# Another table of wanted times for a planned order: four layers of attention and experts on one core

## The chip, the cores and the metric

The kernel runs on one core of one Trainium2 chip. Its time is the device time of one execution in microseconds (us), and versions are compared by the median of several executions. A separate execution was taken with the hardware profiler, which records when each instruction of each engine starts and how long it takes. The engines are called PE (TensorE), DVE (VectorE), ACT (ScalarE), POOL (GpSimd) and SP (SyncE, which in this kernel issues nearly all DMAs).

## The reference

The input x has 64 sequences of 64 tokens of 128 values, the context has 64 sequences of 64 tokens of 96 values, all float32. Four layers follow one another, and each adds two updates to x: a cross-attention to the context and a mixture of experts.

```
for i in 0..3:
    x = x + tanh(g_xattn[i]) * attention_i(layernorm(x), ctx)
    x = x + tanh(g_ffn[i])   * experts_i(layernorm(x))
return x
```

- Layer 0: attention with 16 heads of 8 values; 32 small experts, of which each token takes 6, and a shared expert.
- Layer 1: attention with 16 heads, and a rule that holds for the whole batch: if any weight of the softmax is NaN, all weights become 1/64. Then 8 experts with 256 hidden values, of which each token takes 2, and a shared expert.
- Layer 2: attention with 8 heads of 64 values; 8 experts, two of them per token, and a shared expert.
- Layer 3: a resampler, in which x asks and the keys are the context (masked) and x itself, 2 heads with normalised queries and keys; 4 experts with a layer norm inside, two per token, and a layer norm of the result.

## The kernel before, in words

**Tiles.** The 4096 tokens are 32 tiles of 128, and these are 8 blocks of 512 tokens (`NB`, `TB`, `TOK`, lines 21 to 25). x stays in SBUF for the whole kernel. Work is done block by block: in the main loop (lines 1750 to 1789) each layer's attention or experts for one block is one *stage*. The stages have kinds: "16 heads, 0" and "16 heads, 1" (`attention_16`, line 760), "gated 0" and "gated 2" (`gated_ffn`, line 1340), "end of 16 heads, 1" (line 922), "context, 8 heads" (keys and values of layer 2, line 934), "8 heads" (line 971), "resampler" (`attention_lat`, line 1084), "last" (`ffn_3`, line 1684), and "gated 1" (`sparse_ffn`, line 1527), which takes two blocks at once, so that there are four of it, called groups 0 to 3. The end of layer 1's attention needs the flag of the NaN rule from all 8 blocks; so the first half of the program holds layers 0 and the attention of 1, and the second half the rest.

**Who sets the order.** The body does not issue instructions. It records them in a `Plan` (line 184): every call becomes an operation with an engine, an estimated duration, and what it reads and writes. `stage` (line 218) gives each operation a key, a wanted time that runs from the start to the end named for this stage in the table `TIMES` (lines 49 to 90), in step with the TensorE work in it:

```
op.key = start + (end - start) * done / total
if op.eng == "PE":
    done += op.us
```

`order` (line 288) then plays the program through with its estimates: whenever an engine is free it takes, among the operations that are ready and can hold their buffers, the one with the smallest key (on ACT a change of function table adds 3.0 to the key). At most two stages of a kind are open at a time (`at_once`; the two kinds of 16 heads count together, and so do "gated 0" and "gated 2"). `issue` (line 431) emits the operations in the order of these starts, each into its engine's queue; on the chip each engine runs its queue strictly in that order. As all instructions are emitted at line 435, all rows of the profile say L435, and the tiles' names tell the steps apart. TIMES has 72 pairs (8 per kind, 4 for "gated 1"). They are no promise of times: some of them lie before zero, or end before they start.

**The steps that the prediction names.** A layer norm leaves z (POOL or DVE); PE transposes it into pz, and ACT copies that to zTm or zTs (`normed_T`, line 659). From zT come the projections pq (queries), and pk and pv from the context. sc and sc8 are scores of 16 and 8 heads, pr8 the softmax of "8 heads", whose last step is two multiplications on POOL; pt are transposed softmax rows, av and av8 the attention output, which ACT copies to yT, and po its projection.

In "gated 0", "gated 2" and "last" every token meets every expert with a weight. The routing gives pl (logits), the weights are transposed (pcT), copied by ACT, stored to HBM (cD) and loaded again as rows spread over all partitions (pb; `weights_T` and `spread`, lines 1228 and 1238). g and u are the two hidden matmuls, h = silu(g) * u, weighted by pb on POOL, and acc collects the second matmul. In "last", pg are matmuls with a Gram matrix that give variances (pvar), zs are weighted inputs (DVE, from pb), ph the hidden matmuls, acc3 the sums.

"gated 1" is sparse. After the routing of two blocks, `slots_of` (line 1399) sorts tokens by expert into 24 tiles of 128 slots: PE makes ranks (prank), DVE works on them, PE makes the list of tokens (pid), and DVE writes it as z_rows. The shared expert runs meanwhile (g, u, h, acc). Then, for eight triples of tiles, SP fetches three experts' weights (wt, 384 KB a tile; at most three wt are held), POOL gathers three tiles of tokens (zs, 24 gathers a group), PE transposes them (pt), ACT copies them back to zs, and g, u, h, po follow; the result goes to HBM (oD):

```
for k, j in enumerate(js):
    fetch(wt[:, k, :, :].rearrange("p k w -> p (k w)"), w_rows[0:1, j : j + 1], expert_d)
for k, j in enumerate(js):
    gather(zs[:, k, :], zD, z_rows[:, j : j + 1])
```

At a group's end POOL gathers each token's two results (back, 16 gathers a group), and DVE adds them to x. "8 heads" of the same blocks follows. It loads its keys and values (kT8, v8, 1 MB each), which "context, 8 heads" had stored.

Of the kernel before, what the change touches and what calls it, by code (L numbers as in the profile page):

```python
# [47 lines left out]

TIMES = {
    "16 heads, 0": [  # L50
        (-246, 241.8), (90, 178.8), (206.3, 259), (345.6, 219),
        (400.2, 417.7), (451.6, 497.5), (524.8, 338.3), (616.8, 153.4),
    ],
    "16 heads, 1": [
        (115.4, 151.3), (255.3, 431.1), (-4.4, 256.7), (501.1, 574.1),
        (-154.1, 516.8), (645.4, 766.1), (725.5, 820.9), (327.2, 1815.9),
    ],
    "8 heads": [
        (1810.8, -289.4), (1215.1, 808.1), (1395.5, 939.2), (1485.1, 876.8),
        (756.1, 1010.9), (1771.2, 1176.9), (1150.1, 1706.2), (1641.6, 1363.8),  # L60
    ],
    "context, 8 heads": [
        (-1505.7, -266.7), (1321.7, 960), (268.1, 103.1), (1421.2, 860.9),
        (851.2, 615.6), (1214.3, 1438.8), (1351.2, 821.5), (1428.4, 903.1),
    ],
    "end of 16 heads, 1": [
        (549.1, -654.8), (774.2, -702.6), (2005.6, 1294.3), (527.8, 1272.9),
        (1973.5, 1999.7), (1128.7, 3466.8), (2201.7, 2327.6), (1453, 882.6),
    ],
    "gated 0": [  # L70
        (199, 245.1), (223.9, 304.3), (284.5, 327.4), (374, 492.2),
        (446, 533.4), (593.6, 598.8), (598.3, 694.5), (646.3, 779.7),
    ],
    "gated 1": [
        (-153.1, 570.4), (771.2, 898), (1240.1, 1502.8), (1569.3, 1755),
    ],
    "gated 2": [
        (-544.7, 789.1), (1046.6, 1080.4), (-523.3, 690.8), (-176.3, 1324.9),
        (765.4, 1282.7), (432.2, 1488.7), (111.2, 1616), (1389.7, 2013.7),
    ],  # L80
    "last": [
        (994.7, 1236.8), (1107.1, 1287.4), (1101.4, 1732.7), (853.8, 1150.1),
        (1753.5, 2380.6), (2351, 2461.2), (2622.5, 2971), (-245, -130.7),
    ],
    "resampler": [
        (-824.7, 580.6), (285.1, 510.5), (781.7, 32.2), (1559.7, 1223.5),
        (-1333.4, 131.4), (-54.8, -881.9), (1140.3, 81.7), (-280.5, -1539.5),
    ],
}
AT_ONCE = {}  # L90
# [1797 lines left out]
```

## Time and profile before

| what | value |
|---|---|
| times of five runs | 1733.81, 1726.38, 1719.09, 1724.93, 1730.34 us |
| their median | 1726.38 us |
| time of the profiled execution | 1730.04 us |
| its span, first to last instruction | 1728.3 us |
| mean granted clock of TensorE | 0.961 |
| instructions | 37,328 |
| PE busy | 1587.6 us, 92% of the span, 14,369 matmuls |
| DVE, POOL, ACT busy | 1064.2 (62%), 930.5 (54%), 859.0 us (50%) |
| function table loads on ACT | 159, 204.0 us |
| DMA | 180.94 MB, 105 GB/s in the mean |

"Busy" is the time in which an engine carries out an instruction; what is left of PE's span, 140.7 us, is idle. The page also cuts the span into 40 slices of 43.2 us and gives for each the busy tenths of every engine and the clock that TensorE was granted (9 is 0.9 or more; full speed is 1). A row of the trace names the start, the duration, the engine, the operation, the tile written and the tile read, and in brackets the idle time before it with the engine and tile that ended it. The view of waits sums these by pair: total, number, longest.

### The profile page before, as it was taken

To read this page: it belongs to the slowest core of one execution; us is meant where nothing else is said; L and a number is where in the kernel's file an instruction comes from. 1 tells how busy PE (TensorE), PEld (TensorE's weight loads), DVE (VectorE), ACT (ScalarE), POOL (GpSimd) and SP (SyncE) were. 2 spreads that over 40 slices of the span, in tenths; PEclk is the share of its full clock that TensorE was granted. 3 is DMA by queue.
4 is the path that set the end of the run, shared out by engine and by line. 5 is a ranking of instruction groups with operands and counts; after the bars stand their busy time and mean duration, and the time that the engine had idled before them with its cause. 6 is when DMAs were issued, how large, how long until landed. Compare 5 with 4: busy or idle time off the path is not lost. (4 is left out here: it accounts for less than half of the span.)

```text
span 1728.3 us, 37328 instructions
## 1 busy us (share of the span) xinstructions
PE 1587.6 (92%) x14369; PEld 1095.3 (63%) x14369; DVE 1064.2 (62%) x2933; ACT 859.0 (50%) x1289; POOL 930.5 (54%) x906
## 2 busy tenths in 40 slices
PE   6999999999999999977769599999999999899976
PEld 3556556556566666556758487766767786677654
DVE  4864777786678665761746366684655474675652
ACT  3563776666757575622324264444443553454332
POOL 7464555565654745322373555686554566654741
PEclk9999999999999999987879799999999999999998
DMA  7231160324031321464567362521152323220201
GB/s 233 95 118 60 59 195 23 117 100 118 27 123 33 102 81 55 159 203 118 150 218 212 97 216 53 181 95 57 37 160 88 103 62 109 88 91 2 81 32 38
DMA packets 107786, 180.94 MB, mean 105 GB/s; under 512 B 22964, under 2 KB 53016, under 8 KB 103128
## 3 DMA queue, kind: packets, MB, share of 16 engines
q1 hardware_dynamic: 102488, 168.06, 29.9%
q0 software_dynamic: 5120, 10.50, 2.9%
q8 instruction: 113, 1.85, 0.4%
q14 instruction: 65, 0.53, 0.1%
HBM read 146.71 MB, written 35.26 MB: 105 GB/s over the span
## 5 line engine op out<-in xcount | busy, mean ns | idle before, releaser
L435 DVE TENSOR_TENSOR h<-h,u 128x512 f32<-128x512 f32 x224 | 150.8, 684 | 211.4 <-PE u L435 139.6
L435 POOL TENSOR_TENSOR h<-h,pb 128x512 f32<-128x512 f32 x128 | 161.6, 1276 | 198.1 <-DVE h L435 112.0
L435 ACT ACTIVATE h<-g 128x512 f32<-128x512 f32 x224 | 132.7, 597 | 226.1 <-PE g L435 201.4
L435 ACT ACT_TABLE_LOAD x159 | 204.0, 1283 | 28.6 <-issue 7.5
L435 POOL TENSOR_TENSOR ln_r<-ln_ve,minus_half 128x4 f32<-128x4 f32 x64 | 66.3, 1036 | 216.6 <-DVE ln_ve L435 206.7
L435 PEld LDWEIGHTS acc<-w_L,h 128*128 128x128 f32 x1088 | 134.9, 191 | 42.2 <-issue 30.4
L435 PEld LDWEIGHTS acc<-L_w,h 128*128 128x128 f32 x1088 | 133.5, 192 | 33.8 <-issue 24.1
L435 PE MATMUL acc<-w_L,h 128*128 128x128 f32 x1088 | 144.1, 278 | 0.8 <-POOL h L435 0.6
L435 PE MATMUL acc<-L_w,h 128*128 128x128 f32 x1088 | 142.7, 279 | 1.0 <-DVE h L435 0.4
L435 PE MATMUL g<-zTm,w_L 128*128 128x512 f32 x272 | 141.8, 604 | 0.5 <-ACT cn L435 0.5
L435 PE MATMUL u<-zTm,w_L 128*128 128x512 f32 x272 | 140.1, 599 | 0.0
L435 DVE TENSOR_REDUCE top<-sc 128x16 f32<-128x1024 f32 x80 | 97.4, 1218 | 63.4 <-PE sc L435 32.3
L435 POOL TENSOR_TENSOR kb<-kT,masks 128x1024 f32<-128x1024 f32 x64 | 121.1, 1907 | 23.5 <-ACT kT L435 8.1
L435 POOL DMA_INDIRECT zs<-zD,z_rows x96 | 92.9, 967 | 75.3 <-DVE z_rows L435 23.7
L435 POOL TENSOR_SCALAR z<-x,ln_mv,ln_r 128x128 f32<-128x128 f32 x160 | 128.6, 817 | 4.4 <-DMA zs<-cT 0.7
L435 ACT COPY prT<-pt 128x512 f32<-128x512 f32 x176 | 96.0, 592 | 50.0 <-PE pt L435 44.0
L435 POOL TENSOR_TENSOR pb<-zTm,pb 128x512 f32<-128x512 f32 x64 | 80.1, 1274 | 43.7 <-DMA pb<-cD 43.5
L435 ACT ACTIVATE pr<-pr 128x1024 f32<-128x1024 f32 x88 | 93.0, 1057 | 17.0 <-DVE pr L435 16.2
L435 PEld LDWEIGHTS pt<-masks,pr 128*128 128x128 f32 x704 | 79.9, 142 | 31.8 <-issue 21.7
L435 PE MATMUL pt<-masks,pr 128*128 128x128 f32 x704 | 97.4, 276 | 2.9 <-POOL pr L435 1.1
L435 POOL TENSOR_TENSOR pr<-pr,rs 128x512 f32<-128x512 f32 (+1 forms) x40 | 47.9, 1214 | 80.5 <-DVE rs L435 58.5
L435 POOL DMA_INDIRECT back<-oD,rows_of x64 | 63.5, 992 | 45.1 <-issue 23.8
(299 smaller groups left out, 3382.6 us busy)
## 6 DMA issues: line engine op xcount, KB each, us to landing
wt<-experts SPq DMA_DIRECT2D x96, 384.0 KB
pb<-cD SPq DMA_DIRECT2D x256, 128.0 KB
pb<-cD SPq DMA_DIRECT2D x96, 256.0 KB
k_d<-kS SPq DMA_DIRECT2D x8, 1024.0 KB
v_d<-vS SPq DMA_DIRECT2D x8, 1024.0 KB
kT<-k_d SPq DMA_DIRECT2D x8, 1024.0 KB
v<-v_d SPq DMA_DIRECT2D x8, 1024.0 KB
oD<-zs SPq DMA_DIRECT2D x32, 192.0 KB
```

Source lines behind the costliest of these rows:

```text
L435: bound(*args, **kw)
```

## The change

Only the numbers of `TIMES` differ, in all ten lists; no operation, buffer, cap or estimate is changed. In the two built programs the engines' queues hold the same instructions in another order: of PE's queue 3,242 lines of the comparison differ. The stages follow one another in much the same way; those that move most are "gated 1" of group 2, whose fetches lie over a longer part of the program, blocks 1 and 4 of "context, 8 heads", which change places, "8 heads" of block 4, which comes later, and "resampler" and "last" of blocks 0 and 1, which come earlier.

```diff
--- before.py
+++ after.py
@@ -48,43 +48,43 @@
 
 TIMES = {
     "16 heads, 0": [
-        (-246, 241.8), (90, 178.8), (206.3, 259), (345.6, 219),
-        (400.2, 417.7), (451.6, 497.5), (524.8, 338.3), (616.8, 153.4),
+        (-981.8, 675.8), (109.8, 155), (375.9, 429.8), (469.8, 76.6),
+        (609.5, 634.1), (651.9, 691.8), (684.8, 531.1), (742, 835.4),
     ],
     "16 heads, 1": [
-        (115.4, 151.3), (255.3, 431.1), (-4.4, 256.7), (501.1, 574.1),
-        (-154.1, 516.8), (645.4, 766.1), (725.5, 820.9), (327.2, 1815.9),
+        (388.1, 355.4), (433, 640.2), (-782.2, 832), (489.8, 632.6),
+        (89.8, 230.2), (825.5, 1133.9), (499.3, 1380.3), (967, 2438.9),
     ],
     "8 heads": [
-        (1810.8, -289.4), (1215.1, 808.1), (1395.5, 939.2), (1485.1, 876.8),
-        (756.1, 1010.9), (1771.2, 1176.9), (1150.1, 1706.2), (1641.6, 1363.8),
+        (1849, -134.6), (1156, 1103.6), (1571.3, 987.4), (1654.9, 1235.8),
+        (277.1, 1321.8), (1936.6, 1500), (1692.6, 1685.9), (1664.6, 1403.6),
     ],
     "context, 8 heads": [
-        (-1505.7, -266.7), (1321.7, 960), (268.1, 103.1), (1421.2, 860.9),
-        (851.2, 615.6), (1214.3, 1438.8), (1351.2, 821.5), (1428.4, 903.1),
+        (-1394.6, -56.8), (921.2, 1105.3), (566.9, 540), (2098.3, 1194.2),
+        (1337.8, 537.5), (1652.3, 1829.8), (1428.5, 1419.3), (1830.3, 1550.3),
     ],
     "end of 16 heads, 1": [
-        (549.1, -654.8), (774.2, -702.6), (2005.6, 1294.3), (527.8, 1272.9),
-        (1973.5, 1999.7), (1128.7, 3466.8), (2201.7, 2327.6), (1453, 882.6),
+        (1035.4, -493.6), (1663.3, -250.2), (2304.3, 1263.2), (427.5, 1325.9),
+        (2737.2, 2692.3), (1198.4, 2980), (3276.2, 3447), (1893.5, 904.3),
     ],
     "gated 0": [
-        (199, 245.1), (223.9, 304.3), (284.5, 327.4), (374, 492.2),
-        (446, 533.4), (593.6, 598.8), (598.3, 694.5), (646.3, 779.7),
+        (382.8, 412.9), (400, 458.9), (433.3, 561.6), (580.7, 784.2),
+        (786, 786.3), (796, 823.6), (844, 1006.6), (922.6, 1201.6),
     ],
     "gated 1": [
-        (-153.1, 570.4), (771.2, 898), (1240.1, 1502.8), (1569.3, 1755),
+        (23, 614.4), (853.7, 1199.9), (1467.6, 1666.4), (1611.8, 2014),
     ],
     "gated 2": [
-        (-544.7, 789.1), (1046.6, 1080.4), (-523.3, 690.8), (-176.3, 1324.9),
-        (765.4, 1282.7), (432.2, 1488.7), (111.2, 1616), (1389.7, 2013.7),
+        (-1174.2, 592.7), (1028.2, 1210), (-1063, -77.1), (-209.1, 1903.2),
+        (664.9, 1401.5), (-186, 1462.4), (258.2, 1785.4), (969, 2251),
     ],
     "last": [
-        (994.7, 1236.8), (1107.1, 1287.4), (1101.4, 1732.7), (853.8, 1150.1),
-        (1753.5, 2380.6), (2351, 2461.2), (2622.5, 2971), (-245, -130.7),
+        (1040.8, 1609.3), (764.4, 1162), (1139.6, 1828.6), (961.2, 1421.1),
+        (2664.2, 3012.8), (2405.4, 2773.1), (2182.1, 3751.6), (-15.2, 350.6),
     ],
     "resampler": [
-        (-824.7, 580.6), (285.1, 510.5), (781.7, 32.2), (1559.7, 1223.5),
-        (-1333.4, 131.4), (-54.8, -881.9), (1140.3, 81.7), (-280.5, -1539.5),
+        (-849, -545.3), (846.2, 1029.3), (1006.8, -326.2), (1338.7, 1929.7),
+        (-342.5, 1235.4), (304, -674.6), (1089.7, -35.4), (598.1, -1077.8),
     ],
 }
 AT_ONCE = {}
```

## The prediction

> **What bounds the kernel now.** I read the page's slices first, then the sums by stretch, the waits of PE, and timelines at the places where PE stands still. The two rows that matter of the slices (40 slices of 43.2 us; busy tenths of PE, and the granted clock):
>
> ```profile
> PE   6999999999999999977769599999999999899976
> ...
> PEclk9999999999999999987879799999999999999998
> ```
>
> TensorE is the bound: it is busy 1587.6 of 1728.3 us, nearly without a hole from 43 to 734 us. A new order of the same instructions can win only what is idle, 140.7 us, and what runs at a lower clock. Both lie mainly between 734 and 1000 us, where the sparse layer ("gated 1") begins. Next, the sums over 50 us there (PE busy, PEld, DVE, ACT, POOL, then clock, DMA share, GB/s):
>
> ```profile
> 750.00:800.00 50.00, 34.89 (x208) 30.43 (x204) 20.61 (x43) 8.39 (x17) 18.31 (x19) 0.76 0.50 155
> ...
> 850.00:900.00 50.00, 28.28 (x173) 25.90 (x174) 27.08 (x100) 7.55 (x16) 39.20 (x44) 0.69 0.63 199
> ...
> 950.00:1000.00 50.00, 31.26 (x228) 25.43 (x228) 16.34 (x59) 12.62 (x21) 24.01 (x26) 0.76 0.39 118
> ```
>
> Three of these six windows have 15 to 22 us of idle each; nobody else is full, so it is chains, not an engine, that end last. Whom PE waits for between 730 and 1000 us (total, times, longest):
>
> ```profile
> PE g L435 <- ACT zs L435: 14.1, 4, 11.1
> PE pt L435 <- DMA zs<-zD,z_rows: 11.6, 3, 7.5
> PE pl L435 <- ACT zTm L435: 9.0, 2, 8.7
> PE pid L435 <- issue: 8.5, 1, 8.5
> ...
> PE pid L435 <- DVE h L435: 4.3, 1, 4.3
> ```
>
> These five make 47.5 us. The end has two more holes, before the first hidden matmul of blocks 6 and 7 of "last" (7.91 us here, and 6.82 us at 1703.3):
>
> ```profile
> 1664.97 0.60 PE L435 MATMUL pcT<-masks,cr 128*8 128x128 f32 x4
> 1673.48 3.40 PE L435 MATMUL ph<-zs,L_w 128*128 128x512 f32 x4 [7.91 <-DVE zs L435]
> 1676.71 0.60 PE L435 MATMUL pz<-masks,z 128*128 128x128 f32 x4
> ```
>
> **The change, part by part.** I compared the order of the built programs, which holds no times. The instructions are the same: 8,273 on TensorE in both, 159 table loads on ScalarE in both, the same 96 and 64 gathers, the same transfers. So the work costs what it did; only holes change. I price each named hole by its cover: the PE instructions that stand in the order between the one that starts a chain and the one that waits for it, times their rows.
>
> 1. Start. PE's first 17 units of work, up to the fourth score of block 0, stand unchanged, and until about 50 us of PE work only one transpose changes places with its neighbour: 0.
>
> 2. "gated 0", 43 to 734 us. All idle time of these 16 slices is 10 us, so no order can win more. From the routing transpose (pcT) to the first acc that needs its spread rows, the cover of blocks 2 and 5 grows from 7.6 and 6.8 to 9.3 us; others move by under 3 us either way. The trace has one such wait, 0.6 us at 493 us. I take -0.6, between -10 and +5 (half of the present idle again).
>
> 3. Sparse groups 0 and 1. From the ranks (prank) to the slot matmuls (pid), group 0 had acc, po and four pv as cover, and gets u, po and three pk: 6.9 to 5.8 us, so +1.1 on the 4.3 us wait. In group 1 u (1.08) leaves the cover: +1.1 on 8.5 us. From pid to the first gathered transpose (pt), group 1 gets two more po (1.13 us each): -2.3 of the 11.6 us. In group 0 that cover falls from 9.1 to 7.1 us; the chain took 9.4 us in group 1 (865.07 to 874.47), so +2.0. Sum +1.9, between -10 and +6 (each wait grown by half of its present cover).
>
> 4. The 8.7 us before pl of group 1. The new order puts 8 us of work between pz and pl where 1.7 us stood. Yet ACT copied pz 9.3 us after its recorded end, and DVE took acc 5.4 us after its own: TensorE itself ran behind its records there, beside nine expert loads and 15 gathers. The 24 gathers of group 0, its first expert loads and its 16 "back" gathers stand in rows alike in both orders, so I take 0, between -8.7 and 0.
>
> The Trainium skill, Perfetto Trace Analysis, "Summary: the profiler window per engine type", says that TensorE's end in a profile is an estimate; the 9.3 us above show how far off it can be. By that rule the hole before pl is no dependency that a better order removes (0); by the wait table alone the change would win 8.7 us there.
>
> 5. Sparse group 1's end and group 2. This is the largest hole: g waits 11.1 us until 972.25, then po 2.53 and 1.46 us, with 0.9 at 960.8: 16.0 us. Behind it (ScalarE's rows, start and duration):
>
> ```profile
> 969.33 0.59 ACT L435 COPY yT<-av 128x512 f32<-128x512 f32 x1 [15.48 <-remote]
> ...
> 971.73 0.47 ACT L435 COPY zs<-pt 128x384 f32<-128x384 f32 x1
> ```
>
> zs stands behind a copy of attention output in ScalarE's queue, and meanwhile GpSimd issues 16 "back" gathers in a row, 946.63 to 966.33, 1.25 us apart; the two softmax multiplications of "8 heads" come only after them, and the second pair of transposes waits for those. The new order cuts the row: the longest part left is 11, or 11 x 1.25 = 14 us. Ahead of it in GpSimd's queue now stand all softmax multiplications of block 1 of "8 heads" and all eight multiplications of "gated 2" block 0; behind it only a norm of "resampler" waits, and TensorE has the matmuls of that "gated 2" block as cover. I take half of the hole, -8.0; the bounds are -16 (all goes) and +9 (a hole like that before pl is added). The clock: this slice (950.4 to 993.6) was granted 0.72, 24 us at half speed, with PE busy 57% of it; half of 24 x 0.57 x 0.5 is -3, between -7 and +5.
>
> The Trainium skill, TensorE: Matmul & The Clock Gate, "Terms", puts the penalty of throttled time at that time x (1 - K/N). Summed over the 40 slices, the trace shows some 135 us at half clock, 67 us of penalty by the rule; for this one slice it gives 12 us, half of which is 6 where I took 3, and the sum would be 3 us lower.
>
> 6. "gated 2" and "8 heads" from 1000 to 1640 us. From pcT to g the cover is 7.6 and 3.1 us in blocks 6 and 7 before, 3.0 and 9.9 after: the short one changes its block. 0, between -5 and +8.
>
> 7. The tail. Before, ph of block 6 follows pcT at once. After, pz, pl and four pg of block 7 stand between (5.2 us). But pz needs z, which GpSimd had ready at 1675.46, 9.9 us after pcT's end; then pl waits 0.9 us for the copy of pz. So 10.8 us of idle stand in place of 7.9: +2.9. In return, two ph and two acc (3.9 us) now stand between block 7's pcT and its ph, where 6.8 us were idle: -3.9. Together -1.0, between -4 and +4. The end is unchanged behind that: 15 us of matmuls, the norm, and the store.
>
> Sum: -0.6 + 1.9 + 0 - 8.0 - 3.0 + 0 - 1.0 = -10.7 us. The profiled execution took 1730.0 us (span 1728.3), so 1719.3 on its footing; the median of the five runs is 1726.4, 0.9979 of it, which gives **1716 us**.
>
> What hides the rest: from 43 to 734 us some 680 us of dense matmuls hide DVE, ACT and POOL at 40 to 80% busy. If that cover broke, POOL would be late first: its weighting h<-h,pb takes 1276 ns beside DVE.
>
> **The rivals.** A: TensorE's running behind is set off by the way the gathers and loads are bunched, and the spreading ends it in all places. For it: every such place lies beside a row of gathers. Against it: groups 0 and 1 keep theirs. It wins point 4 (8.7) and the rest of point 5 (8.0) more: 1716 - 17 = 1699.
>
> B: the holes move with the loads and the waits are only exchanged. For it: points 3, 6 and 7 nearly cancel, and the time is set by in-order queues that I did not add up. Without point 5 the sum is +0.3: 1727.
>
> C, slower: block 1 of "8 heads" now runs inside group 1's expert loop, and its 1 MB key load is issued among that group's expert loads. If the keys and experts land late, PE, which is in order, stands before its sc or g as at 772 to 781: one more hole of 8.7, with 13.7 us at half clock after it (6.8), and no gain from point 5: 1730.0 + 0.3 + 15.5 = 1745.8, or 1742. It decides from the point where holes between 890 and 1050 us add up to more than they do now. For it: DMA is 0.77 busy between 900 and 950. Against it: the new order also spreads group 2's expert loads over a stretch nearly twice as long.
>
> **How the numbers follow.** What five runs of this kernel can tell from no change is about 0.5%, 8.6 us, so faster is below 1717.7 and slower above 1735.0. Forecast, 0.42, with a range of its own of 1706 to 1724: 0.27 below 1717.7 and 0.15 within. A 0.14, faster. B 0.18, within. C 0.26, slower. That gives faster 0.41, within 0.33, slower 0.26. The range leaves out a tenth at each end: 1698 (A's time, half of A left out) to 1744 (C's time and a little, a third of C left out).
>
> **What would show it.** Right: the idle before g of group 2 is below 6 us and the slices from 907 to 1037 hold less idle in sum than their 22; pid of group 1 still waits 8 to 11 us, and pl or its neighbours still show a hole near 8 us; the tail shows a hole of about 10 before pz of block 7 and of about 3 before ph. Wrong: a new hole over 5 us between 890 and 1050 (C), none over 5 between 760 and 800 (A), or idle growing from 43 to 734 us, which I hold to be covered.

## The result, and the profile after

The changed kernel takes 1734.47 us (median of 52 runs, 1723.48 to 1748.44), the kernel before 1730.35 us (median of 94, 1718.70 to 1737.67). The ratio is 1.0029, interval 1.0019 to 1.0039: slower by 0.3%, inside the band of half a per cent that I had called no change, and not the 0.6% faster that I forecast. The 1726.4 us on whose footing I forecast was a median of five; with more runs it is 4.0 us higher.

The profiled execution has a span of 1734.0 us (1728.3 before). PE is busy for 1591.6 us (1587.6) and idle for 142.4 us (140.7). The two rows of the slices, of the changed kernel, in tenths as before:

```profile
PE   6999899999999999988779979899989998999977
...
PEclk9999999999999999988979989999999999999988
```

The digits of slices 18 to 23, the sparse groups, are as good or better than before. But a 7 stands in slice 24, where a 9 was, and an 8 now stands in the fifth slice of PE, where 9s stood up to the seventeenth, and a 9 hides up to 4 us of idle time. The waits of PE in the changed kernel (total, times, longest):

```profile
PE sc L435 <- DVE pr L435: 9.6, 6, 5.3
PE pid L435 <- issue: 9.3, 1, 9.3
PE g L435 <- ACT zs L435: 8.6, 3, 7.5
PE pt L435 <- DMA zs<-zD,z_rows: 8.6, 5, 3.5
```

The wait of pl (9.0 before) and the long one of g (11.1) are gone, pt waits 8.6 in place of 12.7, and at the top stands one that was small: sc, the scores of 16 heads, which belong to the first half. So I cut both spans at the first matmul of sparse group 0, the transpose pz. These are the sums by stretch (PE busy, PEld, DVE, ACT, POOL, then clock, DMA share, GB/s): before, then after.

```profile
43.00:734.00 691.00, 680.64 (x6557) 416.51 (x6554) 482.29 (x1076) 441.18 (x626) 373.37 (x325) 1.00 0.28 91
...
896.00:1005.00 109.00, 85.30 (x753) 70.49 (x752) 53.72 (x175) 40.02 (x67) 50.56 (x55) 0.87 0.58 167
```

```profile
43.00:753.00 710.00, 687.52 (x6580) 423.02 (x6577) 492.36 (x1078) 430.84 (x618) 375.28 (x325) 0.99 0.27 90
...
900.00:1021.00 121.00, 114.09 (x1173) 92.45 (x1172) 70.28 (x216) 55.06 (x88) 64.53 (x67) 0.97 0.53 163
```

The two first lines hold nearly the same work (6,557 and 6,580 matmuls) and take 691 and 710 us. The idle time grows from 10.4 to 22.5 us and the clock falls from 1.00 to 0.99, which the clock's rows resolve into 17.1 us at half speed where there was none. Counted by span: up to that pz 733.6 us before and 752.7 after, **+19.1**; behind it 994.7 and 981.3, **-13.4**. The sum, +5.7, is the difference of the two spans.

The place where I put the gain did improve. After, the stretch from the first work of "8 heads" to 1021 us has 6.9 us of idle time (121.00 less 114.09) where 23.7 stood in 109 us. Part of the hole came back later:

```profile
1027.27 0.55 PE L435 MATMUL pt<-masks,zs 128*128 128x128 f32 x3
1035.30 1.65 PE L435 MATMUL g<-zs,wt 128*128 128x128 f32 x6 [7.48 <-ACT zs L435]
```

Later runs fell on two levels: the kernel before took 1736 us beside runs 5 to 8 and 1672 us beside the others, although it is the same program. What sets the level is open: the expectations below speak of slower and faster chips, but the record names chip 10 for runs 5 to 8 and for runs 13 to 16 alike. Every ratio below is to before beside it, as recorded with its 95% interval; it can differ by some 0.002 from the quotient of the two medians.

### The profile page after: what moved, and what is told of

Its sections match the earlier page's. It is cut to its first block, busy times and chain, and to the rows that moved or that the text cites. A ratio compares the mean times of both kernels' runs of the same rounds, so it can differ in the third digit from the quotient of the medians.

```text
span 1734.0 us, 37345 instructions
## 1 busy us (share of the span) xinstructions
PE 1591.6 (92%) x14369; PEld 1102.3 (64%) x14369; DVE 1092.8 (63%) x2933; ACT 857.4 (49%) x1289; POOL 935.5 (54%) x906
## 4 chain that ended last, share of the span: by engine, by line
PE 76%; DVE 8%; issue 4%; POOL 4%; ACT 2%; another core or an unknown queue 2%; DMA 2%; SPq 1%; POOLq 0%; DVEq 0%; ACTq 0%
PE acc L435 14%; PE g L435 13%; PE u L435 12%; PE av L435 6%; PE pt L435 5%; PE po L435 5%; PE sc L435 4%; PE pk L435 3%; PE pv L435 3%; PE ph L435 3%; PE pq L435 2%; DVE top L435 1%; PE pl L435 1%; PE pz L435 1%
## 5 line engine op out<-in xcount | busy, mean ns | idle before, releaser
L435 POOL TENSOR_TENSOR kb<-kT,masks 128x1024 f32<-128x1024 f32 x64 | 121.5, 1913 | 20.3 <-ACT kT L435 15.0
L435 POOL TENSOR_TENSOR pb<-zTm,pb 128x512 f32<-128x512 f32 x64 | 79.6, 1270 | 14.2 <-PE g L435 11.1
L435 PE MATMUL sc<-kb,qT 64*64 64x512 f32 x512 | 71.5, 629 | 10.6 <-DVE pr L435 8.1
```

The source lines that it names most:

```text
L435: bound(*args, **kw)
```

## The experiments

Two theories at the start. **EARLY**: the new order loses in the dense first part and wins from the sparse groups on. **LATE**: the first part only looks different in one profile, and what costs are new holes behind 1020 us. Beneath EARLY stands **PORT**: small DVE instructions are held while POOL works, and what stands behind them in DVE's queue comes late; its rival **CHAIN** says that the holes come from the chains themselves.

**Runs 1 and 2: the two orders spliced.** Both tables are played by the planner; then the first part of one order and all that is left in the other's order are issued, each engine strictly in that sequence. On every engine the order of the first half's operations is exactly that of its parent, and 98 to 100% of neighbours in the second half are the other parent's. (The splices have 163 and 155 function table loads on ACT where both kernels have 159.)

```diff
 def issue(self):
...
+    starts = []
+    for which in range(2):
+        for op in self.ops:
+            op.key = op.keys[which]
+        self.order()
+        starts.append(self.starts)
+    for i, op in enumerate(self.ops):
+        op.key = starts[0][i] if starts[0][i] < 745.0 else 1e4 + starts[1][i]
...
-        for i in self.order():
+        for i in self.order(strict=True):
```

(`keys` are the wanted times by both tables; `strict` lets an engine take only the first of its queue. Run 2 has the tables exchanged and 750 in place of 745.)

> Order of before up to its planned time 745 (until just after the first sparse group begins), order of after for all that is left. Theory EARLY (the new order loses in the dense first half, 12 us of new idle time and 17 us at half clock, and wins about as much from group 0 on): 1713 to 1720 us, faster than both, ratio to before 0.990 to 0.994; the idle time of TensorE from 43 us to the first sparse group stays near 10 us. Theory LATE (the first half only looks different in one profile, the loss is the new holes after 1020 us): 1732 to 1742, ratio 1.001 to 1.007.

Measured: 1668.44 against 1671.90 us, ratio 0.9985 (0.9968 to 1.0002), between the two theories. The idle time from 43 us to the first sparse group is 12.0 us.

> Order of after up to its planned time 750, order of before for all that is left. EARLY: 1744 to 1752 us, slower than both, ratio to before 1.008 to 1.013, idle time from 43 us to the first sparse group over 20 us. LATE: 1722 to 1730, ratio 0.996 to 1.000.

Measured: 1689.09 us, ratio 1.0111 (1.0080 to 1.0141). The idle time up to the sparse group is 22.9 us. The loss of the first part is there in full, as EARLY has it, and LATE falls. But the gain of the rest is much smaller on this level than EARLY expected.

**Runs 3 and 4: without the clip.** The 32 clips are planned and not issued, in the order of after and of before; this leaves out the clip of the row maxima to plus or minus 10000.

```diff
 nc.vector.tensor_scalar(top, top, CLAMP, -CLAMP, op0=ALU.min, op1=ALU.max)
+nc.ops[-1].calls = []
```

> The order of after, but the 32 clips of the row maxima in the second 16-head attention (DVE, 128x16, mostly 0.17 us) are planned and not issued, so the clip to plus or minus 10000 is left out. One of them took 6.66 us in the profile of after, beside a row of POOL products, and TensorE waited 5.29 us for what stood behind it. Theory PORT (the small instruction is held while POOL works): the 5.3 us hole near 196 us goes, with 3 us of half clock: 1724 to 1729 us, 6 to 10 us below after. Rival CHAIN (the wait comes from the scores' own chain, the clip only shows it): the hole stays at 4 us or more, time within 3 us of after, 1732 to 1737.

Measured: 1678.73 us, ratio 1.0053 (1.0032 to 1.0073). The hole of 5.29 us near 196 us is gone; 1.70 us are left, before another tile.

> The order of before without the same 32 clips. PORT: there only three of them took over 1.5 us and the one hole behind them is 1.3 us, so 0 to 3 us below before: 1727 to 1730. CHAIN: the same within 2 us.

Measured: 1666.15 us, ratio 0.9966 (0.9947 to 0.9984). That is 5.75 us, more than either theory allowed: the clip costs as much in the old order, and it isn't what sets the two apart.

**Runs 5 and 6: both kernels again.** No edit.

> The changed kernel as it is, beside the kernel before on the same chip. Expectation from the two halves of the runs above (new first part +17 us, new rest -3.4 us on a chip on which before took 1672 us): there 1.007 to 1.010; on a chip on which before takes 1730 us the rest wins some 15 us, so 1.001 to 1.005. If the halves did not add up (a loss at the seam of the spliced orders), it would be below 1.004 on the faster chip as well.

Measured: 1739.60 against 1736.24 us, ratio 1.0042 (1.0017 to 1.0066), on the slower level, as expected there.

> The kernel before as it is, for its profile on this chip. If the chips differ in the sparse groups alone, idle time of TensorE from 43 us to the first sparse group is near 10 us as in the first profile, and the groups lose less than the 66 us of idle time they lose there.

Measured: 1734.59 us; 10.3 us of idle time from 43 us to group 0, as in the first profile. On this level the groups lose what they lost there.

**Run 7: the splice with two instructions exchanged.** In the splice of run 1, TensorE waits 5.61 us before pvar in block 2 of "last". DVE in that splice:

```profile
1204.62 6.59 DVE L492 TENSOR_TENSOR c<-m,sm 128x16 f32<-128x16 f32 x1
1211.13 0.67 DVE L492 TENSOR_TENSOR q<-zTs,pg 128x512 f32<-128x512 f32 x1
```

and POOL:

```profile
1205.03 6.14 POOL L492 TENSOR_TENSOR pb<-zTm,pb 128x512 f32<-128x512 f32 x5
```

c is a product of 16 values a partition. Its neighbours of the same kind take 0.18 us, and it takes 6.59, until POOL's five products are through. q, for which pvar waits, stands behind it. The edit puts q first:

```diff
+        seq = self.order(strict=True)
+        seq.remove(3784)
+        seq.insert(seq.index(3776), 3784)
-        for i in self.order(strict=True):
+        for i in seq:
```

> The old first part with the new rest, and two DVE instructions of block 2 of the last layer changing places: the product q3 that reads PSUM, for which pvar waits, goes ahead of the four small ones that normalise the weights, the last of which (c) took 6.59 us beside five POOL products. PORT: the 5.6 us hole before pvar goes and 1 to 3 us come back later as the queue behind c is still held: 3 to 6 us below the splice without the swap, ratio to before 0.994 to 0.997. Rival (DVE is late there anyway): the hole stays, ratio 0.998 to 1.000.

Measured on the slower level: 1733.70 us, ratio 0.9998 (0.9977 to 1.0018), where the rival had it. The hole before pvar is gone, and sm, another small instruction, is held for 6.00 us. Run 17 repeats it. Run 7 says one thing more, which I take up below: on this level the old first part with the new rest is no faster than before.

**Run 8: products ahead of gathers.** In the order of before, two softmax products of block 0 of "8 heads" stand behind 16 back gathers in POOL's queue. They are put behind the third.

```diff
+        seq = self.order()
+        for k in (2844, 2843):
+            seq.remove(k)
+            seq.insert(seq.index(2842) + 1, k)
-        for i in self.order():
+        for i in seq:
```

> The order of before, but the two softmax products of block 0 of the 8 heads go ahead of thirteen of the sixteen back gathers in POOL's queue; nothing else moves. Theory QUEUE (the hole at the start of group 2 is the row of gathers in front of those products): the hole before pt near 940 us (6.4 us, on the slower chip 11 us before g at 972 us) shrinks below 2 us, and the time falls by 5 to 10 us, ratio 0.994 to 0.997. Rival LAG (TensorE itself is late there, beside gathers and expert loads): hole and time stay, ratio 0.998 to 1.002.

Measured: 1737.90 us, ratio 1.0015 (0.9992 to 1.0038): no gain. The wait for the products is gone, and a longer one stands in its place, in PE and then ACT:

```profile
969.61 0.83 PE L439 MATMUL u<-zs,wt 128*128 128x128 f32 x6
990.27 3.03 PE L439 MATMUL po<-wt,hs 128*128 128x128 f32 x12 [19.83 <-DVE hs L439]
```

```profile
983.92 0.49 ACT L439 ACTIVATE hs<-g 128x384 f32<-128x384 f32 x1 [9.33 <-remote]
989.67 0.49 ACT L439 ACTIVATE hs<-g 128x384 f32<-128x384 f32 x1 [5.26 <-remote]
```

The matmuls of g and u are recorded as done by 970.4 us, but ACT, idle since 974.6, can take the first g only at 983.9; the trace has the update of TensorE's semaphore that it waited for at 983.90. TensorE itself was late by some 14 us. POOL issued gathers without a break from 958.4 to beyond 984.9 us, 1.25 us apart.

**Runs 9 and 10: the splices again**, unchanged.

> The splice with the old first part and the new rest, once more beside before, because chips differ. If the two halves add up on every chip: on one where before takes 1730 us, 0.993 to 0.997 (the new order as a whole 1.003 to 1.004, less 0.010 for its first part); where before takes 1670 us, 0.997 to 1.000 as measured. If the gain in the sparse groups hangs on when they start, and not on their order alone: 0.998 to 1.001 on the slower chip too, as with the swap (0.9998).

Measured: 1667.62 against 1672.37 us, ratio 0.9974 (0.9962 to 0.9985).

> The reverse splice once more. EARLY: 1.008 to 1.013 on either chip, with over 20 us of idle time between 43 us and the first sparse group. If the first part costs only on the faster chip: under 1.005 on the slower one.

Measured: 1689.55 us, ratio 1.0117 (1.0087 to 1.0147). The idle time up to the sparse group is 19.1 us, just under the 20 expected. Both runs fell on the faster level, as in runs 1 and 2, so the question about the slower one stayed.

**Runs 11 and 12: the back gathers replaced.** In the order of before, by a memset, or by a product with zero and a memset. Both leave the routed experts' results of layer 1 out of x.

```diff
 gather(back[:, t, :], oD, rows_of[:, k, i * TB + t : i * TB + t + 1])
+nc.ops[-1].calls = [(tc.nc.gpsimd.memset, (back[:, t, :], 0.0), {})]
```

> The order of before, but each of the 64 back gathers is issued as a short POOL memset, so the experts' results of layer 1 are left out of x (the shared expert stays). Theory GATHER (TensorE runs slowly while POOL issues gathers in a row, on the slower chip): ratio 0.980 to 0.992 there, and the slow rows of TensorE between 940 and 990 us go; on the faster chip 0.993 to 0.998. Theory QUEUE (only the POOL products behind the row wait): 0.993 to 0.997 on both. Theory LOADS (the expert loads slow TensorE): 0.997 to 1.001 on both.

Measured: 1661.39 against 1672.37 us, ratio 0.9932 (0.9911 to 0.9953).

> As the run before this one, but each back gather is replaced by a POOL product with zero of 128x128 and a memset, some 1.0 us of the 1.25 us that a gather holds POOL's queue; the experts' results of layer 1 are left out as well. GATHER: within 0.003 of the run with memsets alone, as it is the gathers themselves that matter. QUEUE: 0.998 to 1.001, as POOL's queue is as long as before. LOADS: 0.997 to 1.001, as with memsets.

Measured: 1666.30 us, ratio 0.9961 (0.9949 to 0.9973). Both remove the 6.4 us hole before pt of "8 heads" (which the old order shows on this level in run 4, at 939.3 us), and LOADS is out here by run 11. The two are apart by 0.0029 with intervals that overlap. They don't part GATHER from QUEUE: the product and the memset together took POOL some 0.77 us and not the 1.0 that I had reckoned, so a row of 16 was 7.7 us shorter, more than the hole. Both also leave out the gathers' transfers, and no run separates these from the row. They fell on the faster level, where TensorE doesn't fall behind, so they say nothing on the 14 us.

**Runs 13 to 16: all four on one level.** The changed kernel, the same without the clip, and both splices.

> The changed kernel once more. ADDITIVE (the parts add up on each chip): where before takes 1670 us, 1.008 to 1.011 (the two splices gave 1.011 and 0.998 there); where it takes 1730 us, 1.002 to 1.006 as already measured twice. If the parts do not add up: under 1.006 on the faster chip.

Measured: 1683.12 against 1671.65 us, ratio 1.0073 (1.0056 to 1.0089).

> The changed kernel without the 32 clips (left out: the clip to plus or minus 10000) beside the changed kernel itself. PORT: 0.003 to 0.006 lower than it in ratio, on either chip, with the 5.3 us hole near 196 us gone. CHAIN: within 0.0015.

Measured: 1680.60 us, ratio 1.0046 (1.0029 to 1.0063): 0.0027 below the run before, with intervals that overlap, so neither theory is hit cleanly. And in run 13 itself the 5.29 us hole is missing though the clip is there: the hold falls on an instruction that stands two places behind it (pr, 4.89 us). So the missing hole of run 3 can't be put down to the clip that was left out.

> Old first part, new rest. ADDITIVE: on the slower chip 0.990 to 0.996, as the sparse groups lose more there before; on the faster one 0.997 to 0.999 as before. Otherwise 0.998 to 1.001 on the slower chip.

Measured: 1668.72 us, ratio 0.9980 (0.9969 to 0.9992).

> New first part, old rest. ADDITIVE: 1.008 to 1.013 on either chip. If the first part's loss is made good later on the slower chip: under 1.006 there.

Measured: 1688.72 us, ratio 1.0093 (1.0067 to 1.0120). The parts add up: three times new first part 1.0111, 1.0117, 1.0093, mean 1.0107, and new rest 0.9985, 0.9974, 0.9980, mean 0.9980, give 1.0087, inside the interval of the whole.

**Runs 17 and 18: runs 7 and 8 on the other level.**

> The splice of old first part and new rest with the two DVE instructions swapped. Where before takes 1670 us: PORT 0.993 to 0.997, as the 5.6 us hole before pvar goes and the splice alone gave 0.998 three times; rival (what is held shows in the next wait) 0.997 to 0.999. Where before takes 1730 us: 0.998 to 1.002 as before.

Measured: 1669.67 against 1673.06 us, ratio 0.9983 (0.9970 to 0.9996): nothing more than the splice alone. DVE shows why:

```profile
1205.96 0.68 DVE L495 TENSOR_TENSOR q<-zTs,pg 128x512 f32<-128x512 f32 x1
1206.56 0.16 DVE L495 TENSOR_REDUCE sm<-m 128x4 f32<-128x16 f32 x1
1206.75 6.54 DVE L495 TENSOR_SCALAR sm<-sm 128x4 f32<-128x4 f32 x1
```

q runs now in 0.68 us and the hole before pvar is gone. POOL's five products start at 1207.11 and take 6.15 us, and the instruction that stands there at that moment, a different one, is held for 6.54 us. The accumulation behind it in DVE's queue comes late in its turn, and g of "gated 2" waits 5.89 us.

> The order of before with the two softmax products ahead of thirteen gathers. Where before takes 1670 us: QUEUE 0.994 to 0.997, the 6.4 us hole before pt near 940 us under 2 us; LAG 0.998 to 1.001 with a new hole behind the gathers. Where before takes 1730 us: 0.999 to 1.003 as before.

Measured: 1674.40 us, ratio 1.0012 (0.9999 to 1.0025). The hole before the products is gone here too, and PE waits for the next in POOL's queue, the gathers of group 2's tokens, which stand behind the same 16:

```profile
952.01 0.45 PE L439 MATMUL pt<-masks,zs 128*128 128x128 f32 x1 [8.32 <-DMA zs<-zD,z_rows]
```

So both QUEUE and LAG had a part wrong: the row is the bottleneck, and not the products alone.

## Why the prediction was wrong

The forecast was a gain of 10.7 us; the two profiles differ by +5.7 us in span. **The step that failed is point 2**: "All idle time of these 16 slices is 10 us, so no order can win more", -0.6 with an upper end of +5. It measured +19.1 us. The bound of the gain was right, and that of the loss (half of the present idle time) was no bound: that a stretch is dense says what an order can win there and nothing of what it can lose. I priced the cover of one kind of chain (pcT to acc), and the holes came from others: 1.5 us before pz at 81 us, 5.3 before sc at 196, 3.2 before pcT itself at 311, 2.4 before pt at 432, 1.4 before u at 474, 2.1 before acc at 480, 1.3 before sc at 732. These are 17.2 of the 22.5 us; all but the second recur in all three profiles of the changed kernel, and that one in two of them. Idle time is one part of the loss, and the clock is the other: 6.8, 6.8 and 3.4 us at half speed come with the holes at 81, 196 and 311. PE is idle for 12.1 us more and busy for 6.9 us more in this stretch, which are the 19 us; half of the 17.1 us at half speed, 8.5, is my estimate of the clock's share.

That this is the order of the first part is shown by the splices, three times each way. The first matmul of group 0 starts at 732.4 to 739.5 us in the eleven profiles with the whole old first part and at 749.3 to 756.9 us in the six with the new one, on both levels. Idle time from 43 us to there is 9.1 to 12.1 us in the first set and 19.1 to 22.9 in the second; time at half speed is none in the first and 13.7 to 27.3 us in the second.

What delays the chains is read from rows, for three of the seven places. At 196 us, DVE and POOL of the changed kernel:

```profile
186.63 1.22 DVE L435 TENSOR_REDUCE top<-sc 128x16 f32<-128x1024 f32 x1 [2.10 <-ACT pr L435]
187.89 6.66 DVE L435 TENSOR_SCALAR top<-top 128x16 f32<-128x16 f32 x1
194.58 1.23 DVE L435 SCALAR_TENSOR_TENSOR pr<-sc,top 128x1024 f32<-128x1024 f32 x1
```

```profile
187.60 1.27 POOL L435 TENSOR_TENSOR h<-h,pb 128x512 f32<-128x512 f32 x1
188.81 0.19 POOL L435 MEMSET sp<- 128x32 f32 x2
188.95 1.27 POOL L435 TENSOR_TENSOR h<-h,pb 128x512 f32<-128x512 f32 x1
190.18 1.90 POOL L435 TENSOR_TENSOR kb<-kT,masks 128x1024 f32<-128x1024 f32 x1
192.03 2.48 POOL L435 TENSOR_TENSOR h<-h,pb 128x512 f32<-128x512 f32 x2
```

An instruction that mostly takes 0.17 us starts in the middle of a row of POOL products and ends when the row ends, at 194.5. The scores' buffer is read by the instruction behind it, so the next scores wait. At 81 us four DVE instructions z take 6.01 us beside three POOL products kb of 5.62, and at 311 sm and c take 1.78 and 1.95 beside kb again. In each of the three changed profiles four DVE instructions take over 3 us in this way; in the seven profiles in the order of before none does. A hold need not cost: the second of the four, 4.24 us at 524 us, left no hole over 0.7 us near it. The planner forbids the two at the same time, but there a free engine takes other work; on the chip the queue is fixed, and what stands behind the held one waits with it.

At 196 us the eight profiles with the new first part (two of them without the clip) decide it. In four of them (the changed kernel, runs 2, 5 and 16) the clip is held, for 6.66 us, ahead of the instruction that reads the scores, and the hole of 5.29 us is there. In the other four (runs 3, 10, 13 and 14) the row holds the instruction behind that reader, pr, for 4.88 to 5.94 us, and in place of that hole 1.7 us are left, before pt. DVE and PE in run 13:

```profile
188.19 1.02 DVE L435 TENSOR_SCALAR top<-top 128x16 f32<-128x16 f32 x1
189.24 1.23 DVE L435 SCALAR_TENSOR_TENSOR pr<-sc,top 128x1024 f32<-128x1024 f32 x1
190.50 4.89 DVE L435 TENSOR_SCALAR pr<-pr 128x1024 f32<-128x1024 f32 x1
```

```profile
190.89 1.09 PE L435 MATMUL sc<-kb,qT 64*64 64x512 f32 x8
196.53 1.09 PE L435 MATMUL pt<-masks,pr 128*128 128x128 f32 x8 [1.71 <-ACT pr L435]
```

So the hole comes and goes with which instruction the row holds, which speaks for PORT and against CHAIN there. At 81 and 311 us the cause is only read from rows that overlap. Runs 7 and 17 show the hold itself, which passes to whatever stands in its place; leaving out the clip could not show it at 196 us, as the hold is on pr without the clip too (run 3). The other four places have no held instruction in sight (at 432 us DVE waits 3.67 us for weights from HBM), and I did not test them. The three places have 10.1 of the 17.2 us, and all the time at half speed in this profile stands with them.

The Trainium skill, SBUF — State Buffer, "Who interferes with whom", says that DVE and GpSimd share a pair of ports as an exclusive lock, for the whole instruction of whoever comes first. The holds fit a lock, but not one of a single instruction's length: in run 1 c was held for 6.59 us, five POOL products and not one. DVE's record starts there 0.4 us ahead of the products (1204.62 and 1205.03); POOL was then in the gather before them (1204.06 to 1205.01), beside which the two DVE instructions ahead of c took 0.17 and 0.18 us, so what held c at its start is open.

The rule of the same skill, TensorE: Matmul & The Clock Gate, "Terms", that throttled time costs about that time x (1 - K/N), gives 8.5 us for 17.1 us at half clock, as an estimate. PE's busy time in this stretch grew by 6.9 us.

Point by point, the rest:

- **Point 1, the start**: right. 15.2 and 15.3 us of idle time.
- **Points 3 and 4, groups 0 and 1**: +1.9 forecast; idle time from the first pz to "8 heads" falls from 42.4 to 36.2 us, so a gain of about 6, inside the bounds. pid waits 5.3 us in group 0 and 9.3 us in group 1, where the covers gave 5.4 and 9.6. The hole before pl is gone, which I had put at nothing; 2.7 before g, 2.4 before po and 1.9 us before pt stand nearby.
- **Point 5, group 2**: -11.0 forecast with the clock. From the start of "8 heads" to the first work of "resampler" the idle time falls by 17.5 us (24.4 to 6.9), and the time at half clock from 27 to 6 us. (The two stretches, 162 and 106 us long, don't hold the same work.) But 7.5 us came back before g at 1035, and I had said below 6. The size came out, the reason is not shown: I had put half of the hole down to the products behind the row of gathers, and in run 8, with two of them ahead of the row in the old order, a longer hole stood in its place, behind a late TensorE. The copy yT that I quoted from ScalarE's rows (idle 15.48 us before it) is such a lag as well: its av is recorded as done at 951.8, and TensorE's semaphore rises at 969.3. Between 1006 and 1505 us the idle time is 34.1 us, where the like stretch had 20.3.
- **Point 6**: 0 forecast, bounds -5 to +8; this +13.8 contains the returned hole and 2.7 us before pvar behind a held c (6.58 us); the others are under 2.7 us each.
- **Point 7, the tail**: -1.0 forecast. Idle time 19.6 before and 19.0 after from 1505 us on, but 34 us at half clock in place of 18. z of block 7 did hold pz (4.8 us and not 10), and ph of block 7 waits 3.4 (3 said).

Taken together, the rest from the first matmul of group 0 on gave -13.4 us in this pair of profiles and -15.4 in runs 5 and 6, a little more than my -10.1 for points 3 to 7. That its new order alone wins this is not shown on this level. In run 7 the new rest stands behind the old first part, with an exchange that changed nothing in run 17, and there it took 995.8 us, like the old rest (994.7 and 997.3) and not 981 to 982. So point 2 is the loss that the profiles show, but undoing it did not bring the forecast gain, and why is open. On the faster level the new rest gave some 7 us in the profiles (934.7 to 938.4 us with the old rest, 927.8 to 929.9 with the new one) and 3 to 5 us in the medians of the splices; there is less idle time to win there.

The rivals: A (1699) is out, the lag did not end; the 7.5 us before g at 1035 are again a copy on ACT that waits 6.01 us for a transpose recorded as done. B (1727) came nearest in size, with +0.3 us where C had +15.8 and the spans +5.7: waits are exchanged, and runs 8, 17 and 18 each show one that moved to the next in line. Its reason, in-order queues that I did not add up, fits these rows, but I saw it only in the sparse groups. C did not happen: no hole of its size stands in group 1's expert loop.

My own list of signs named the failing one: "idle growing from 43 to 734 us, which I hold to be covered". Of the others, idle time from 907 to 1037 us did fall, from 22 to 14.7 us; but the 7.5 us before g at 1035 are also the sign that I had set for C, though they stand in group 2 and not where C has its hole.

**A version better than both** is the splice of old first part and new rest: ratios 0.9985, 0.9974 and 0.9980, of which two have intervals below 1. It is worth 0.2% on the faster level; on the slower one only its form with the exchange ran (0.9998).

## What to carry to other kernels

A dense stretch bounds what a new order can win in it and not what it can lose: price every kind of chain that ends at the full engine, and don't take the present idle time for an upper end (here 10.4 us became 22.5, and the clock fell too). Where an engine's queue holds a long row (16 gathers, five products), moving one victim ahead of it shows the next: the row itself has to be shorter (runs 11 and 12, with results left out, won 0.7 and 0.4% that way). When an order as a whole moves the time little, splice it with the old one at a seam and measure both halves; here +1.1% and -0.2% stood behind +0.7% on one level. Measure them on the level that the forecast is for: on the other the halves were not shown to add up.

## What the runs showed of the hardware that I had not expected

- A DVE instruction on SBUF operands of 4 to 16 values a partition can be held through a whole row of POOL products: 6.54 to 6.66 us where others of its kind take 0.17 or 0.18. One of 1024 values was held as well (pr, 4.88 to 5.94 us, 0.69 without). Products h<-h,u, which read PSUM, were not: 22 of them started inside POOL products between 43 and 753 us of the changed profile, and took 0.67 to 0.69 us.
- The same program took 1672 and 1736 us, 3.8% apart, in different groups of runs. In the order of before the first matmul of group 0 differs little (734 us in run 18, 732 in run 8); from there to the end it is 937 and 1005 us, and the idle time from there to "8 heads" is 24.6 and 42.6 us.
- On the slower level TensorE fell some 14 us behind its recorded ends beside unbroken rows of gathers (run 8); the same program on the faster level (run 18) has the same row and no such wait, and 8.3 us before the gathered tokens in its place. The cause is open: runs 11 and 12, meant for it, fell on the faster level.
